# Two-layer attention kernel: the end of the first finished batch, the last stage and the bounds' check in another order, and its block of x1 asked for on another queue

## The chip, the core and the metric

The kernel runs on one core of one Trainium2 chip, in one launch. The metric is the device time of a run in microseconds (us); the median of several runs is compared. The trace of one profiled execution says what each engine did: TensorE (PE, with its weight loads as PEld), VectorE (DVE), ScalarE (ACT), GpSimd (POOL) and SyncE (SP), which here only issues DMAs.

## What is computed

The input x has two batches of 512 channels and 64 x 32 = 2048 tokens, in fp32. Cut to what matters (8 heads of 64):

```python
# layer 0
qk = concat([x, embedding])                  # 512 + 64 channels
q, k, v = qk @ Wq, qk @ Wk, x @ Wv           # tokens x 512
x1 = x + softmax(q k^T / 8) v @ Wout + bout  # full attention, 2048 x 2048 a head
# layer 1: attention by 256 landmarks (mean of 8 tokens each: qL, kL)
t = layer_norm(x1)
q, k, v = split(t @ Wqkv)
a1, a2, a3 = softmax(q kL^T), softmax(qL kL^T), softmax(qL k^T)
o = a1 @ (pinv(a2) @ (a3 @ v)) + conv33(v)   # pinv: 6 rounds of an iteration
t = x1 + o @ Wout + bout
out = t + layer_norm(t) @ (W @ dequantized).T
```

## The kernel before

Everything is kept with channels on the 128 partitions and tokens along the row: a batch is four blocks of 512 tokens (NTB = 4), each block four rows of channels (KC = 4). Heads go in pairs of two (NPAIR = 4 pairs a batch), so layer 1 has eight pairs; `todo` lists batch 1's four first, then batch 0's, and the text counts them n = 0 to 7.

**Order of work.** The instructions of PE, DVE, ACT and POOL run in the order in which the program writes them: each engine takes the next when its waits are met, and everything behind a waiting one on the same engine waits too. Only SP's order is the planner's. The program is written as generators that yield at places where something else may go between; `advance` (L793) takes one step of the next generator in a list, and a yielded `GAP` (`gap(n)` yields n of them) means that a generator sits out a turn, so that its next matmul isn't placed right behind the work that it needs. Results of matmuls go to PSUM banks; `bank` hands out four in turn, and a matmul into a bank waits for the reader of what stood there before.

**Layer 0's start** (L820 to 943). The weights and x are loaded on SP, the embedding (`emb_f`, 64 x 96) by two DMAs on POOL after VectorE has cleared it, and the embedding's weights (`we`) of the first chunk on ACT's queue. Twenty warm-up matmuls run meanwhile. For each of q and k of the first pair of heads, a matmul forms the embedding's part as 64 + 32 columns, VectorE copies it (`ft`, L888), POOL spreads it over 64 x 32 tokens (`e`, L889) and SP keeps it in memory (L895) for batch 1. VectorE adds e to each of the four projected blocks (L905). The buffer of e is one, for q and k in turn.

**Landmark scores** (`attend`, L1268). For each of the four pairs of a batch, two heads: two matmuls each into one half of a two-bank tile `sc2` (L1280), exp on ACT into X (L1287), sums and division on VectorE. POOL sets the last column of X to one (L1275). Pairs with i < 3 share one tile for the two heads.

**Pseudo-inverses** (the loop over `todo`, `pinv` at L1525). Five rounds of products of 256 x 256 matrices for two heads: a flip (a transpose at L1522 and a copy on ACT at L1523), products at L1532, combinations on VectorE (`less`, L1545), then three steps with transposed products (`wp` L1507, `tp` L1516). Each round is followed by `chunk(c)` and each of the last six half steps by `last(i)`: these put other work between, so that PE doesn't stand still. That other work is: for the pair before, the output of its four token blocks (`attn1_*`, L1581 to 1626: scores, exp, an addition `acc` L1598, values `av`, sums `rs`, a reciprocal L1618, a spread by eight DMAs on SP L790, a multiplication by it on VectorE L1625 and an addition to o on POOL L1626); for the pair after, its `attn3`, landmarks and start; the values of the pair after that; and `finish`.

**A batch's end** (`Finish1`, L1628; `finish1_units`, L1692). For each block t: x1 is read back into `xb` by four DMAs on SP (L1637). `out_units` project o (`yp`, L965) and add bias and x1 on VectorE (L972). `norm_units` takes the steps of `statistics` (L980): partial sums (L983, L984), a matmul for the mean and its subtraction `xn` (L988), squares on ACT (L991, L994) and their sums on VectorE (L996, L997), a matmul for the variance (L1000), root and reciprocal. `map_units` multiplies by the folded feed-forward map (`fp`, L1682), scales (L1671), adds (L1672) and stores each quarter on SP (L1673). Batch 1's blocks use one `xb` and one `xn` buffer, so block t + 1 can be read only when block t's four stores are done. Batch 1's end is appended to `finish` after pair n = 4 and is advanced in the chunks of pairs 5 to 7.

**The last stage.** After pair 7, a string (L2040) sets the order: `f` is a unit of batch 1's end, `1` a step of pair 7's output, `a` and `b` units of the projection of batch 0's blocks 0 and 1, `s` and `t` steps of their statistics. Batch 0's blocks have buffers of their own. Then the bounds' check: `halves` is set by three memsets on POOL (L2054 to 2056), a matmul sums the collected bounds (`bp`, L2058), three VectorE operations compare them and POOL reduces over the partitions (`bad`, L2064). At the very end `bad` is read (L2102, L2103), and if a bound is too large the whole is computed again in a safer way, which doesn't happen with these inputs. Last, batch 0's four blocks go through `map_units`, with the statistics of the next and the projection of the next but one between.

Of the kernel before, what the change touches and what calls it, by code (L numbers as in the profile page):

```python
# [663 lines left out]
def fast_path(  # L664
# [154 lines left out]


    emb_sb = wpool0.tile([64, H + W], F32, name="emb_f")
    nc.vector.memset(emb_sb, 0.0)
    w_sb = {kind: wpool0.tile([P, KC, C], F32, name=f"w{kind}_f") for kind in "qk"}
    we = {kind: wpool0.tile([64, C], F32, name=f"we{kind}_f") for kind in "qk"}

    def load_w0(kind, cols, queue=nc.sync):
        w = {"q": wq0, "k": wk0}[kind]
        nc.sync.dma_start(w_sb[kind][:, :, cols], chunked(w[:C, cols]))
        queue.dma_start(we[kind][:, cols], w[C:, cols])

    nc.gpsimd.dma_start(emb_sb[:32, :H], freq)
    nc.gpsimd.dma_start(emb_sb[32:, H:], time)
    load_w0("q", slice(0, P), nc.scalar)

    def load_x(src, b, name, first=0, n=NTB):
        tiles = []
# [21 lines left out]
    class Heads0:  # L858
# [12 lines left out]
        def embedded_and_projected(self, kind):  # L871

            cols, xbs = self.cols, self.xbs
            if kind == "q":
                self.q = qopool.tile([P, S], F32, tag="qo", name=f"q_{self.name}")

            def embedded(kind):


                e = wpool0.tile([P, H, W], F32, tag="e", name=f"e_{kind}_{self.name}")  # L880
                flat, kept = e.rearrange("p h w -> p (h w)"), e_d["qk".index(kind), self.hp]
                if self.b:
                    nc.sync.dma_start(flat, kept)
                    return flat
                fp = bank(f"fp_{kind}_{self.name}")
                nc.tensor.matmul(fp[:, : H + W], lhsT=we[kind][:, cols], rhs=emb_sb, start=True, stop=True)
                ft = wpool0.tile([P, H + W], F32, tag="ft", name=f"ft_{kind}_{self.name}")
                nc.vector.tensor_copy(ft, fp[:, : H + W])  # L888
                nc.gpsimd.tensor_tensor(  # L889
                    e,  # L890
                    ft[:, :H].unsqueeze(2).to_broadcast([P, H, W]),
                    ft[:, H:].unsqueeze(1).to_broadcast([P, H, W]),
                    ALU.add,
                )
                nc.sync.dma_start(kept, flat)  # L895
                return flat

            def project(kind, dst, e, t):
                toks = slice(t * TB, (t + 1) * TB)
                pp = bank(f"pp_{kind}_{self.name}_{t}")  # L900
                for k in range(KC):
                    nc.tensor.matmul(  # L902
                        pp, lhsT=w_sb[kind][:, k, cols], rhs=xbs[t][:, k, :], start=k == 0, stop=k == KC - 1
                    )
                nc.vector.tensor_tensor(dst[:, toks], pp, e[:, toks], ALU.add)  # L905

            dst = self.q if kind == "q" else self.k
            e = embedded(kind)
            if self.b:
                yield from gap(2)  # L910
            else:
                yield
                yield GAP
            for t in range(NTB):
                project(kind, dst, e, t)
                yield
# [60 lines left out]
    def deviation(name):  # L977
        return apool.tile([P, TB], F32, tag="rstd", name=f"rstd_{name}", bufs=1)

    def statistics(xb, xn, part, name, squares, row):  # L980


        nc.vector.tensor_tensor(part, xb[:, :2, :], xb[:, 2:, :], ALU.add)  # L983
        nc.vector.tensor_tensor(part[:, 0, :], part[:, 0, :], part[:, 1, :], ALU.add)  # L984
        yield
        mean = bank(f"mean_{name}")
        nc.tensor.matmul(mean, lhsT=mean_w, rhs=part[:, 0, :], start=True, stop=True)  # L987
        nc.vector.tensor_tensor(xn, xb, mean.unsqueeze(1).to_broadcast([P, KC, TB]), ALU.subtract)  # L988
        yield
        sq, *others = squares()  # L990
        nc.scalar.activation(sq, xn[:, :2, :], AF.Square)  # L991
        n = 2 // len(others)
        for i, other in enumerate(others):
            nc.scalar.activation(other, xn[:, 2 + i * n : 2 + (i + 1) * n, :], AF.Square)  # L994
            to = sq[:, i * n : (i + 1) * n, :]
            nc.vector.tensor_tensor(to, to, other, ALU.add)  # L996
        nc.vector.tensor_tensor(sq[:, 0, :], sq[:, 0, :], sq[:, 1, :], ALU.add)  # L997
        yield
        var = bank(f"var_{name}")
        nc.tensor.matmul(var, lhsT=mean_w, rhs=sq[:, 0, :], start=True, stop=True)  # L1000
        rstd = row()
        nc.scalar.activation(rstd, var, AF.Sqrt, bias=eps, scale=1.0)
        yield rstd
# [204 lines left out]
    class Pair:  # L1208
# [59 lines left out]
        def attend(self):  # L1268

            i, L = self.i, self.L  # L1270
            scs = scores_bank(f"sc2_{i}") if i + 1 < NPAIR else None
            X = self.X = [zpool.tile([P, 2, LM + 1], F32, tag=f"M{h}", name=f"X_{i}_{h}") for h in range(2)]
            rs = small.tile([P, 4], F32, tag="rs2", name=f"rs2_{i}")
            for h in range(2):
                nc.gpsimd.memset(X[h][:, :, LM:], 1.0)  # L1275
            for h in range(2):
                rows_h = slice(h * D, (h + 1) * D)
                sc = scs[:, h, :] if scs is not None else bank(f"sc2_{i}_{h}")
                for t in range(2):
                    nc.tensor.matmul(  # L1280
                        sc[:, t * LM : (t + 1) * LM],
# [346 lines left out]
    class Finish1:  # L1628

        def __init__(self, b, t, os, xb, xn):
            self.b, self.t, self.os, self.xb, self.xn = b, t, os, xb, xn
            self.name = f"g_{b}_{t}"
            toks = slice(t * TB, (t + 1) * TB)
            for m in range(KC):
                nc.sync.dma_start(xb[:, m, :], chunked(x1_d[b])[:, m, toks])  # L1637

        def out_units(self):
            return residual_units(self.b, self.t, self.xb, self.os, wo_sb, b1_sb, self.name)  # L1640

        def steps(self, row):
            def squares():
                sq = apool.tile([P, 2, TB], F32, tag="acc", name=f"sq_{self.name}")
                return sq, *(row_of(f"sq{k}_{self.name}").unsqueeze(1) for k in (2, 3))

            self.xn = self.xn()
            for rstd in statistics(self.xb, self.xn, self.xn[:, :2, :], self.name, squares, row):
                if rstd is not None:
                    nc.vector.reciprocal(rstd, rstd)  # L1650
                    self.rstd = rstd
                yield

        def norm_units(self):
            steps = self.steps(lambda: deviation(self.name))
            next(steps)
            yield GAP
            next(steps)
            yield
            next(steps)  # L1660
            yield from gap(2)
            next(steps)
# [29 lines left out]
    def finish1_units(b, os):  # L1692
        for t in range(NTB):
            xb = block_of(lpool, "xr", f"xb_g_{b}_{t}")
            f = Finish1(b, t, os, xb, lambda: block_of(lpool, "xn", f"xn_g_{b}_{t}"))
            yield from f.out_units()
            yield from f.norm_units()
            yield from f.map_units(lambda m, name: bank(name))
# [184 lines left out]
            next(first, None)  # L1883
    drain(first)
    todo[1].prefetch_w()
    vals = [values(1)]
    advance(vals)
    for n in todo[NPAIR - 1].front():
        advance(vals, n // 2)
    start_scale()  # L1890
    todo[0].prefetch1(kvpool.tile([P, S], F32, tag="k", name="q2_first"))


# [2 lines left out]
    for n, pair in enumerate(todo):  # L1896
# [20 lines left out]
        def chunk(c):  # L1917
            nonlocal landmarks
            if before and 0 < c <= n_ones:
                before.attn1_end(c - 1)  # L1920
            advance(finish)
            if c == NTB:
                if after:
# [64 lines left out]
        landmarks = start = None  # L1988
        n_ones = NTB if n + 2 < len(todo) else NTB - 1
        pair.pinv(chunk, last)  # L1990
        if n == NPAIR:
            finish.append(finish1_units(1, [p.o for p in todo[:NPAIR]]))

    def last_attn1():
        pair, ended = todo[-1], []
        for t in range(NTB):
            for j in range(2 if t else 0):
                pair.attn1_scores(t, j)
                if ended:
                    pair.attn1_end(ended.pop())  # L2000
                yield
            pair.attn1_add(t)
            pair.attn1_values(t)
            yield
            pair.attn1_sums(t)
# [10 lines left out]
        return Finish1(0, t, [p.o for p in todo[NPAIR:]], xb, xn)  # L2016


    fs = [last_block(t) for t in range(NTB)]

    def turns(units, *others):

        for other in others:
            next(units if other is None else other)
        drain(units)

    outs = [f.out_units() for f in fs]

    def deviation_of(t):
        def row():  # L2030
# [3 lines left out]
        return row  # L2034


    st = [f.steps(deviation_of(t)) for t, f in enumerate(fs)]

    ones_last = last_attn1()
    for c in "f1f1f1f1f1f1f1fa1a1a1as11bs1bs1bbt":  # L2040
        if c == "f":
            advance(finish)
        else:
            next({"1": ones_last, "a": outs[0], "b": outs[1], "s": st[0], "t": st[1]}[c])
    assert not finish
    drain(ones_last)
    todo[-1].attn1_end(NTB - 1)
    drain(outs[1])
    next(st[0])

    n = 3 * B * NPAIR

    halves = row_of("halves_f")[:, :P]
    nc.gpsimd.memset(halves, 0.0)  # L2054
    nc.gpsimd.memset(halves[:D, :D], 1.0)
    nc.gpsimd.memset(halves[D:, D:], 1.0)
    bp = bank("bp_f")
    nc.tensor.matmul(bp[:, :n], lhsT=halves, rhs=bound, start=True, stop=True)  # L2058
    ok = small.tile([P, n], F32, name="ok_f")
    nc.vector.tensor_scalar(ok, bp[:, :n], SAFE, None, ALU.is_lt)  # L2060
    oks = small.tile([P, 1], F32, name="oks_f")
    nc.vector.tensor_reduce(oks, ok, AX.X, ALU.min)
    nc.vector.tensor_scalar(oks, oks, -1.0, 1.0, ALU.mult, ALU.add)
    nc.gpsimd.partition_all_reduce(bad, oks, P, bass_isa.ReduceOp.max)  # L2064

    for t in range(NTB):
        maps = fs[t].map_units(wide_banks, 1 if t + 1 < NTB else 2)
        if t + 1 < NTB:
# [96 lines left out]
```

## Time and profile before

| what | value |
|---|---|
| median of 3 runs | 2764.85 us (2764.79 to 2766.75) |
| the profiled execution's own time | 2763.73 us |
| its span, first to last instruction | 2761.9 us |
| mean granted TensorE clock | 0.995 |
| busy: PE, PEld | 2703.8, 1363.3 us |
| busy: DVE, ACT, POOL | 1629.0, 905.8, 164.7 us |
| last matmul ends | 2754.09 us |
| x1 read back, quarter of a block (SP, 256 KB) | lands after 4.2 us |
| a whole block of 1 MB, from POOL | lands after 5.0 us |

The page gives each engine's busy time in the span, then groups of instructions by line. A line such as `L1084 DVE TENSOR_TENSOR acc_f<-acc_f,p_f ... x448 | 582.6, 1300 | 208.8 <-ACT ...` reads: line of the kernel, engine, operation, output and inputs, how many, then busy time in us and the mean of one in ns, then the engine's idle time just before them and what ended most of it. A view of waits lists, for an engine, what ended its idle time: the total, how often, the longest. A timeline gives start and length of each instruction in us from the span's start; idle time before it stands in brackets with what ended it. A stretch's line gives each engine's busy time in it and the TensorE clock that was granted, as a share of full speed.

### The profile page before, as it was taken

Reading aid. Unit: us, or ns where it says so; the run is one execution under the profiler, and the core shown is the slowest. Engines: PE = TensorE matmul, PEld = TensorE weight load, DVE = VectorE, ACT = ScalarE, POOL = GpSimd, SP = SyncE. Lnnn points to the kernel's source line nnn. Section 1 sums busy time; section 2 is a strip of 40 time slices with the busy share of each in tenths; the row PEclk is TensorE's granted clock in tenths of the full one; section 3 lists DMA queues with packets and bytes.
Section 4 is the critical chain, followed back from the end, with each engine's and each line's share of the span. In section 5 each row is a group of like instructions: output and inputs, shape, how many; then the busy total and the mean of one; then the engine's idle time right before and its main releaser. Section 6 shows DMA issues by size and latency. Waiting matters only on the chain. (4 is left out here: it accounts for less than half of the span.)

```text
span 2761.9 us, 41236 instructions
## 1 busy us (share of the span) xinstructions
PE 2703.8 (98%) x16994; PEld 1363.3 (49%) x16994; DVE 1629.0 (59%) x2068; ACT 905.8 (33%) x1352; POOL 164.7 (6%) x125
## 2 busy tenths in 40 slices
PE   9999999999999999999999999999999999899898
PEld 5343443434443334343344465777667767555334
DVE  2768787765558756657657444544644545556465
ACT  1434343433335334344512222223332323221210
POOL 1101101000001100000011000000000000000000
PEclk9999999999999999999999999999999999999999
DMA  4100000212111210021035532213111202111301
GB/s 145 42 9 24 28 20 26 83 35 69 32 66 54 96 39 9 21 73 41 24 107 187 187 121 90 95 32 126 43 36 59 81 9 90 40 64 31 107 31 47
DMA packets 112661, 174.00 MB, mean 63 GB/s; under 512 B 16320, under 2 KB 68048, under 8 KB 107856
## 3 DMA queue, kind: packets, MB, share of 16 engines
q1 hardware_dynamic: 107968, 154.46, 17.3%
q0 software_dynamic: 4416, 16.79, 1.6%
q8 instruction: 135, 2.21, 0.3%
q14 instruction: 62, 0.51, 0.1%
q10 hardware_dynamic: 80, 0.03, 0.0%
HBM read 90.87 MB, written 63.57 MB: 56 GB/s over the span
## 5 line engine op out<-in xcount | busy, mean ns | idle before, releaser
L1084 DVE TENSOR_TENSOR acc_f<-acc_f,p_f 128x1024 f32<-128x1024 f32 x448 | 582.6, 1300 | 208.8 <-ACT p_f L1074 180.2
L1074 ACT ACTIVATE p_f<-sc_f 128x1024 f32<-128x1024 f32 x512 | 496.4, 1021 | 564.2 <-PE sc_f L1066 561.5
L1066 PE MATMUL sc_f<-q_f,k_f 64*64 64x512 f32 x4096 | 491.1, 594 | 2.7 <-ACT p_f L1074 2.7
L1096 PE MATMUL av_f<-p_f,v_f 64*64 64x512 f32 x4096 | 484.3, 589 | 0.0
L1096 PEld LDWEIGHTS av_f<-p_f,v_f 64*64 64x64 f32 x4096 | 156.5, 133 | 283.0 <-issue 283.0
L1066 PEld LDWEIGHTS sc_f<-q_f,k_f 64*64 64x64 f32 x4096 | 145.8, 133 | 285.6 <-issue 262.0
L1239 PE MATMUL pp<-xh,w 128*128 128x512 f32 x512 | 231.0, 603 | 0.7 <-ACT q L1242 0.7
L1239 PEld LDWEIGHTS pp<-xh,w 128*128 128x128 f32 x512 | 95.8, 192 | 122.2 <-issue 115.0
L1532 PE MATMUL pb<-R 128*128 128x192 f32 (+1 forms) x640 | 151.1, 383 | 1.6 <-DVE M L1545 1.6
L1532 PE MATMUL pa<-M 128*128 128x192 f32 (+1 forms) x640 | 150.7, 380 | 0.1
L950 PEld LDWEIGHTS vp_f<-wv_f,x 128*128 128x128 f32 x1024 | 115.7, 192 | 13.5 <-issue 11.8
L950 PE MATMUL vp<-w,xh 128*128 128x128 f32 x1024 | 120.8, 276 | 0.0
L950 PEld LDWEIGHTS vp<-w,xh 128*128 128x128 f32 x1024 | 117.0, 192 | 7.2 <-issue 4.2
L1532 PEld LDWEIGHTS pb<-R 128*128 128x128 f32 x640 | 107.7, 192 | 25.1 <-DVE M L1545 2.3
L950 PE MATMUL vp_f<-wv_f,x 128*128 128x128 f32 x1024 | 118.7, 277 | 0.0
L1532 PEld LDWEIGHTS pa<-M 128*128 128x128 f32 x640 | 108.0, 193 | 21.0 <-ACT M L1523 2.5
L902 PE MATMUL pp_q_f<-x,wq_f 128*128 128x512 f32 x256 | 114.4, 599 | 2.1 <-DVE q_f L905 1.4
L965 PE MATMUL yp_g<-o,wo_f 128*128 128x512 f32 x256 | 115.5, 598 | 0.8 <-DVE y_g L1671 0.8
L902 PE MATMUL pp_k_f<-x,wk_f 128*128 128x512 f32 x256 | 114.3, 599 | 1.7 <-DVE k_f L905 1.3
L1682 PE MATMUL fp_g<-xn_g,mT 128*128 128x512 f32 (+1 forms) x264 | 115.7, 589 | 0.0
L965 PE MATMUL yp_f<-q_f,wo_f 128*128 128x512 f32 x256 | 113.7, 598 | 0.9 <-DVE xr_f L972 0.9
L1114 POOL TENSOR_TENSOR q_f<-q_f,rinv_f 128x512 f32<-128x512 f32 x32 | 44.4, 1387 | 1041.9 <-DMA rinv_f<-acc_f 850.7
(196 smaller groups left out, 2719.3 us busy)
## 6 DMA issues: line engine op xcount, KB each, us to landing
xh<-xh_fd SPq DMA_DIRECT2D x12, 1024.0 KB, 5.6
rinv_f<-acc_f SPq DMA_DIRECT2D x256, 32.0 KB, 1.8
xr_f<-in_x_dram SPq DMA_DIRECT2D x8, 1024.0 KB, 5.2
x_fd<-xr_f POOLq DMA_DIRECT2D x8, 1024.0 KB, 5.0
xh_fd<-xn_f POOLq DMA_DIRECT2D x8, 1024.0 KB, 4.6
k_fd<-k SPq DMA_DIRECT2D x32, 256.0 KB, 2.6
q_fd<-q SPq DMA_DIRECT2D x32, 256.0 KB, 3.1
xb_g<-x_fd SPq DMA_DIRECT2D x32, 256.0 KB, 4.2
```

The lines of the kernel that those rows point to most:

```text
L902: nc.tensor.matmul(pp, lhsT=w_sb[kind][:, k, cols], rhs=xbs[t][:, k, :], start=k == 0, stop=k == KC - 1)
L950: nc.tensor.matmul(vp[:, j * P : (j + 1) * P], lhsT=xb[:, k, j * P : (j + 1) * P], rhs=w_of(k), start=k == 0, stop=k == KC - 1,)
L965: nc.tensor.matmul(yp, lhsT=wo_sb[:, k, m * P : (m + 1) * P], rhs=oTs[k][:, toks], start=k == 0, stop=k == NPAIR - 1,)
L1066: nc.tensor.matmul(sc[r * D : (r + 1) * D, h, :], lhsT=hd.k[rows, lo : lo + D], rhs=hd.q[rows, t * TB : (t + 1) * TB], start=True, stop=True,)
L1074: nc.scalar.activation(p, sc, AF.Exp, scale=D**-0.5)
L1084: nc.vector.tensor_tensor(acc, first if c == 1 else acc, p, ALU.add)
L1096: nc.tensor.matmul(av[r][half, :], lhsT=hd.v[keys, c, half], rhs=pp[keys, h, :], start=c == 0, stop=c == NST - 1,)
L1114: nc.gpsimd.tensor_tensor(o, o, rinv, ALU.mult)
L1239: nc.tensor.matmul(pp, lhsT=self.w[j][:, c, :], rhs=xhs[t][:, c, :], start=c == 0, stop=c == KC - 1)
L1532: nc.tensor.matmul(dst, lhsT=lhsT[:, k, t * P : (t + 1) * P], rhs=rhs[:, k, :], start=k == 0, stop=k == 1)
L1682: nc.tensor.matmul(fp[:, cols], lhsT=mT[:, k, m * P : (m + 1) * P], rhs=self.xn[:, k, cols], start=k == 0, stop=k == KC - 1,)
```

## The change

1. **Start.** `emb_f` is cleared only in the two quarters that no DMA writes. The first chunk of wq, `we` and the embedding's two DMAs all go to ACT's queue, in this order (before: SP, ACT and POOL).
2. **e** of the first pair of heads of batch 0 (for q and for k) is made by VectorE rather than by POOL.
3. **Statistics** get `apart`, used by batch 1's end: a yield between the squares on ACT and their additions on VectorE, and all of ACT's squares are issued before the first addition.
4. **attend** takes two score tiles, one for each head, for i < 3, and X's last column is set by VectorE.
5. **Batch 1's end** reads a block of x1 by one DMA of 1 MB on POOL, and sits out two turns before its projection. The turns sat out in `norm_units` are moved: two after the partial sums, one after the squares.
6. **Order.** Batch 1's end begins in chunk 1 of pair 4 rather than after pair 4. The string of the last stage is another; a letter `n` in it makes batch 0's last blocks with their reads of x1, and the addition `acc` of pair 7's output comes right after its scores.
7. **The bounds' check** moves from the end to around `start_scale`, before the loop over the pairs: memsets before the last values and `front`, matmul and VectorE operations before `start_scale`, the reduction right after it.

```diff
--- before.py
+++ after.py
@@ -819,18 +819,19 @@
 
 
     emb_sb = wpool0.tile([64, H + W], F32, name="emb_f")
-    nc.vector.memset(emb_sb, 0.0)
+    nc.vector.memset(emb_sb[:32, H:], 0.0)
+    nc.vector.memset(emb_sb[32:, :H], 0.0)
     w_sb = {kind: wpool0.tile([P, KC, C], F32, name=f"w{kind}_f") for kind in "qk"}
     we = {kind: wpool0.tile([64, C], F32, name=f"we{kind}_f") for kind in "qk"}
 
     def load_w0(kind, cols, queue=nc.sync):
         w = {"q": wq0, "k": wk0}[kind]
-        nc.sync.dma_start(w_sb[kind][:, :, cols], chunked(w[:C, cols]))
+        queue.dma_start(w_sb[kind][:, :, cols], chunked(w[:C, cols]))
         queue.dma_start(we[kind][:, cols], w[C:, cols])
 
-    nc.gpsimd.dma_start(emb_sb[:32, :H], freq)
-    nc.gpsimd.dma_start(emb_sb[32:, H:], time)
     load_w0("q", slice(0, P), nc.scalar)
+    nc.scalar.dma_start(emb_sb[:32, :H], freq)
+    nc.scalar.dma_start(emb_sb[32:, H:], time)
 
     def load_x(src, b, name, first=0, n=NTB):
         tiles = []
@@ -886,7 +887,9 @@
                 nc.tensor.matmul(fp[:, : H + W], lhsT=we[kind][:, cols], rhs=emb_sb, start=True, stop=True)
                 ft = wpool0.tile([P, H + W], F32, tag="ft", name=f"ft_{kind}_{self.name}")
                 nc.vector.tensor_copy(ft, fp[:, : H + W])
-                nc.gpsimd.tensor_tensor(
+
+                engine = nc.gpsimd if self.b or self.hp else nc.vector
+                engine.tensor_tensor(
                     e,
                     ft[:, :H].unsqueeze(2).to_broadcast([P, H, W]),
                     ft[:, H:].unsqueeze(1).to_broadcast([P, H, W]),
@@ -977,7 +980,7 @@
     def deviation(name):
         return apool.tile([P, TB], F32, tag="rstd", name=f"rstd_{name}", bufs=1)
 
-    def statistics(xb, xn, part, name, squares, row):
+    def statistics(xb, xn, part, name, squares, row, apart=False):
 
 
         nc.vector.tensor_tensor(part, xb[:, :2, :], xb[:, 2:, :], ALU.add)
@@ -992,6 +995,9 @@
         n = 2 // len(others)
         for i, other in enumerate(others):
             nc.scalar.activation(other, xn[:, 2 + i * n : 2 + (i + 1) * n, :], AF.Square)
+        if apart:
+            yield
+        for i, other in enumerate(others):
             to = sq[:, i * n : (i + 1) * n, :]
             nc.vector.tensor_tensor(to, to, other, ALU.add)
         nc.vector.tensor_tensor(sq[:, 0, :], sq[:, 0, :], sq[:, 1, :], ALU.add)
@@ -1268,14 +1274,14 @@
         def attend(self):
 
             i, L = self.i, self.L
-            scs = scores_bank(f"sc2_{i}") if i + 1 < NPAIR else None
+            scs = [scores_bank(f"sc2_{i}_{h}")[:, 0, :] for h in range(2)] if i + 1 < NPAIR else None
             X = self.X = [zpool.tile([P, 2, LM + 1], F32, tag=f"M{h}", name=f"X_{i}_{h}") for h in range(2)]
             rs = small.tile([P, 4], F32, tag="rs2", name=f"rs2_{i}")
             for h in range(2):
-                nc.gpsimd.memset(X[h][:, :, LM:], 1.0)
+                nc.vector.memset(X[h][:, :, LM:], 1.0)
             for h in range(2):
                 rows_h = slice(h * D, (h + 1) * D)
-                sc = scs[:, h, :] if scs is not None else bank(f"sc2_{i}_{h}")
+                sc = scs[h] if scs else bank(f"sc2_{i}_{h}")
                 for t in range(2):
                     nc.tensor.matmul(
                         sc[:, t * LM : (t + 1) * LM],
@@ -1629,34 +1635,40 @@
 
 
 
-        def __init__(self, b, t, os, xb, xn):
+        def __init__(self, b, t, os, xb, xn, t_by_t=False):
             self.b, self.t, self.os, self.xb, self.xn = b, t, os, xb, xn
             self.name = f"g_{b}_{t}"
             toks = slice(t * TB, (t + 1) * TB)
+            if t_by_t:
+
+                nc.gpsimd.dma_start(xb, chunked(x1_d[b])[:, :, toks])
+                return
             for m in range(KC):
                 nc.sync.dma_start(xb[:, m, :], chunked(x1_d[b])[:, m, toks])
 
         def out_units(self):
             return residual_units(self.b, self.t, self.xb, self.os, wo_sb, b1_sb, self.name)
 
-        def steps(self, row):
+        def steps(self, row, apart=False):
             def squares():
                 sq = apool.tile([P, 2, TB], F32, tag="acc", name=f"sq_{self.name}")
                 return sq, *(row_of(f"sq{k}_{self.name}").unsqueeze(1) for k in (2, 3))
 
             self.xn = self.xn()
-            for rstd in statistics(self.xb, self.xn, self.xn[:, :2, :], self.name, squares, row):
+            for rstd in statistics(self.xb, self.xn, self.xn[:, :2, :], self.name, squares, row, apart):
                 if rstd is not None:
                     nc.vector.reciprocal(rstd, rstd)
                     self.rstd = rstd
                 yield
 
         def norm_units(self):
-            steps = self.steps(lambda: deviation(self.name))
+            steps = self.steps(lambda: deviation(self.name), True)
+            next(steps)
+            yield from gap(2)
+            next(steps)
+            yield
             next(steps)
             yield GAP
-            next(steps)
-            yield
             next(steps)
             yield from gap(2)
             next(steps)
@@ -1692,7 +1704,8 @@
     def finish1_units(b, os):
         for t in range(NTB):
             xb = block_of(lpool, "xr", f"xb_g_{b}_{t}")
-            f = Finish1(b, t, os, xb, lambda: block_of(lpool, "xn", f"xn_g_{b}_{t}"))
+            f = Finish1(b, t, os, xb, lambda: block_of(lpool, "xn", f"xn_g_{b}_{t}"), True)
+            yield from gap(2)
             yield from f.out_units()
             yield from f.norm_units()
             yield from f.map_units(lambda m, name: bank(name))
@@ -1883,11 +1896,26 @@
             next(first, None)
     drain(first)
     todo[1].prefetch_w()
+
+
+    halves = row_of("halves_f")[:, :P]
+    nc.gpsimd.memset(halves, 0.0)
+    nc.gpsimd.memset(halves[:D, :D], 1.0)
+    nc.gpsimd.memset(halves[D:, D:], 1.0)
     vals = [values(1)]
     advance(vals)
     for n in todo[NPAIR - 1].front():
         advance(vals, n // 2)
+    n_bounds = 3 * B * NPAIR
+    bp = bank("bp_f")
+    nc.tensor.matmul(bp[:, :n_bounds], lhsT=halves, rhs=bound, start=True, stop=True)
+    ok = small.tile([P, n_bounds], F32, name="ok_f")
+    nc.vector.tensor_scalar(ok, bp[:, :n_bounds], SAFE, None, ALU.is_lt)
+    oks = small.tile([P, 1], F32, name="oks_f")
+    nc.vector.tensor_reduce(oks, ok, AX.X, ALU.min)
+    nc.vector.tensor_scalar(oks, oks, -1.0, 1.0, ALU.mult, ALU.add)
     start_scale()
+    nc.gpsimd.partition_all_reduce(bad, oks, P, bass_isa.ReduceOp.max)
     todo[0].prefetch1(kvpool.tile([P, S], F32, tag="k", name="q2_first"))
 
 
@@ -1918,6 +1946,9 @@
             nonlocal landmarks
             if before and 0 < c <= n_ones:
                 before.attn1_end(c - 1)
+            if n == NPAIR and c == 1:
+
+                finish.append(finish1_units(1, [p.o for p in todo[:NPAIR]]))
             advance(finish)
             if c == NTB:
                 if after:
@@ -1988,18 +2019,18 @@
         landmarks = start = None
         n_ones = NTB if n + 2 < len(todo) else NTB - 1
         pair.pinv(chunk, last)
-        if n == NPAIR:
-            finish.append(finish1_units(1, [p.o for p in todo[:NPAIR]]))
 
     def last_attn1():
         pair, ended = todo[-1], []
+        pair.attn1_add(0)
         for t in range(NTB):
             for j in range(2 if t else 0):
                 pair.attn1_scores(t, j)
                 if ended:
                     pair.attn1_end(ended.pop())
+                if j:
+                    pair.attn1_add(t)
                 yield
-            pair.attn1_add(t)
             pair.attn1_values(t)
             yield
             pair.attn1_sums(t)
@@ -2016,15 +2047,11 @@
         return Finish1(0, t, [p.o for p in todo[NPAIR:]], xb, xn)
 
 
-    fs = [last_block(t) for t in range(NTB)]
-
     def turns(units, *others):
 
         for other in others:
             next(units if other is None else other)
         drain(units)
-
-    outs = [f.out_units() for f in fs]
 
     def deviation_of(t):
         def row():
@@ -2034,35 +2061,23 @@
         return row
 
 
-    st = [f.steps(deviation_of(t)) for t, f in enumerate(fs)]
-
     ones_last = last_attn1()
-    for c in "f1f1f1f1f1f1f1fa1a1a1as11bs1bs1bbt":
+    for c in "11ffnf11f1ff1afafff1f1f1f1faas11bs1bs1bbt":
         if c == "f":
             advance(finish)
+        elif c == "n":
+
+            fs = [last_block(t) for t in range(NTB)]
+            outs = [f.out_units() for f in fs]
+
+            st = [f.steps(deviation_of(t)) for t, f in enumerate(fs)]
         else:
-            next({"1": ones_last, "a": outs[0], "b": outs[1], "s": st[0], "t": st[1]}[c])
+            next(ones_last if c == "1" else {"a": outs[0], "b": outs[1], "s": st[0], "t": st[1]}[c])
     assert not finish
     drain(ones_last)
     todo[-1].attn1_end(NTB - 1)
     drain(outs[1])
     next(st[0])
-
-    n = 3 * B * NPAIR
-
-    halves = row_of("halves_f")[:, :P]
-    nc.gpsimd.memset(halves, 0.0)
-    nc.gpsimd.memset(halves[:D, :D], 1.0)
-    nc.gpsimd.memset(halves[D:, D:], 1.0)
-    bp = bank("bp_f")
-    nc.tensor.matmul(bp[:, :n], lhsT=halves, rhs=bound, start=True, stop=True)
-    ok = small.tile([P, n], F32, name="ok_f")
-    nc.vector.tensor_scalar(ok, bp[:, :n], SAFE, None, ALU.is_lt)
-    oks = small.tile([P, 1], F32, name="oks_f")
-    nc.vector.tensor_reduce(oks, ok, AX.X, ALU.min)
-    nc.vector.tensor_scalar(oks, oks, -1.0, 1.0, ALU.mult, ALU.add)
-    nc.gpsimd.partition_all_reduce(bad, oks, P, bass_isa.ReduceOp.max)
-
     for t in range(NTB):
         maps = fs[t].map_units(wide_banks, 1 if t + 1 < NTB else 2)
         if t + 1 < NTB:
```

## The prediction

> **What bounds the kernel now.** I read the page first: the engines' shares, then the waits of TensorE, the chain of work that ended last, and the timelines around each gap. The first line of the page:
>
> ```profile
> PE 2703.8 (98%) x16994; PEld 1363.3 (49%) x16994; DVE 1629.0 (59%) x2068; ACT 905.8 (33%) x1352; POOL 164.7 (6%) x125
> ```
>
> TensorE is busy for 2703.8 of 2761.9 us, so the work itself leaves 58 us to win: about 50 in gaps and 7.8 after the last matmul (2754.09). The change adds and removes no matmul. So only TensorE's idle time counts, and the view of its waits lists it (total, times, longest):
>
> ```profile
> PE p_pb L1522 <- DVE R L1545: 7.2, 2, 6.8
> PE sc L1280 <- ACT X L1287: 6.2, 3, 3.5
> PE rs L779 <- DVE acc L1598: 5.1, 1, 5.1
> PE bp_f L2058 <- POOL halves_f L2056: 4.9, 1, 4.9
> PE mean_g L987 <- DVE xn_g L984: 3.0, 1, 3.0
> PE wp L1507 <- DVE R L1545: 2.4, 2, 1.6
> PE pp_q_f L902 <- DVE q_f L905: 1.4, 2, 0.9
> PE pp_k_f L902 <- DVE k_f L905: 1.3, 1, 1.3
> ```
>
> The first names VectorE, but its timeline shows that VectorE itself stood still for a load of x1 (idle before it in brackets):
>
> ```profile
> 2389.65 0.75 DVE L972 SCALAR_TENSOR_TENSOR xb_g<-yp_g,b_f,xb_g 128x512 f32<-128x512 f32 x1 [10.39 <-DMA xb_g<-x_fd]
> 2390.32 0.74 DVE L1545 SCALAR_TENSOR_TENSOR R<-M,pa 128x320 f32<-128x320 f32 x2
> ```
>
> A gap costs more than itself. In stretches of 4 us (fields after the engines: TensorE's clock, then DMA), after the gaps of 6.8, 5.1 and 4.9:
>
> ```profile
> 2391.00:2395.00 4.00, 3.55 (x9) 2.67 (x10) 2.05 (x7) 0.27 (x1) 0.00 (x0) 0.50 0.00 2
> 2395.00:2399.00 4.00, 4.00 (x16) 2.53 (x15) 2.11 (x5) 0.27 (x1) 0.30 (x1) 0.99 0.00 2
> 2596.00:2600.00 4.00, 3.17 (x12) 0.86 (x14) 2.39 (x2) 1.70 (x3) 0.00 (x0) 0.57 0.93 354
> 2664.00:2668.00 4.00, 3.69 (x7) 1.63 (x8) 1.97 (x4) 0.00 (x0) 0.22 (x2) 0.59 0.00 0
> ```
>
> Half clock for about 3.4 us is 1.7 us lost. All six gaps of 2.0 us or more (at 1489.6, 1528.8, 2384.1, 2520.5, 2591.8, 2659.4: 3.5, 2.0, 6.8, 3.0, 5.05, 4.95) show it; none up to 1.58 does. Together they hold 25.2 us of idle time and 10.5 of slow clock. The last is in the chain:
>
> ```profile
> 2661.65 0.70 DVE rinv L1625
> ...
> 2662.48 1.25 POOL o L1626
> 2663.73 0.15 POOL halves_f L2054
> ...
> 2664.31 0.40 PE bp_f L2058 x2
> 2664.72 5.22 PE fp_g L1682 x8
> ```
>
> The check's matmul waits for three memsets that queue on POOL behind an addition, which waits for a DMA; the eight matmuls behind it take 5.22 us, where such eight take 3.43 at full clock.
>
> [...] here L988 (128x2048, one operand broadcast) takes 2.28. [...] In the trace x1's block costs four issues of 0.43 us on SP and lands 4.2 us after one; 1 MB from POOL takes 5.0.
>
> **Start** (page, POOL and VectorE timelines). e for q takes 3.63 us on POOL, 12.84 to 16.46, though its input is ready at 8.69. On VectorE, idle there, it ends near 8.7 + 2.3 = 11.0, long before TensorE wants the bank at 16.30: the gap of 0.94 goes. e for k can't start before the store of the first lands (29.21); on VectorE it ends at 31.5 rather than 32.84, and its addition at 32.2, before TensorE needs the bank at 32.29: 1.33 goes. wq, we and the embedding move to ACT's queue, and x is asked for one issue earlier on SP; the bytes are the same, so the 0.60 for x stays. If the embedding, now fourth on its queue, landed after the warm-up (7.94) it would cost; it has some 4 us. Sum -2.3 (-2.9 to -0.5).
>
> **Attend** (three pairs). The second head's scores wait for the first head's exp in the same tile, behind a key copy, two squares and a table load of 1.28 on ACT. Two tiles end that. The gaps are 0.7, 3.5 + 1.7 and 2.0 + 1.7. In the second the next matmul, the variance, needs VectorE's chain, which runs without a break until 1496.84; I take a third of it, -1.7 (-0.8 to -2.6). With -0.7 and -3.7: -6.1 (-7.5 to -4). The two memsets of X cost VectorE about 0.1 each, beside its slack.
>
> **Bounds' check.** At the end -4.95 and -1.65; the matmul's 0.4 moves along. In its new place it is followed by TensorE's 64 value matmuls (1739.2 to 1746.3), while the matrix it waits for is ready at 1742.7: 3.6 us cover the three small VectorE operations (0.5) and the reduction on POOL (0.38). With that cover gone they would cost 0.9. Its memsets are issued early, past no waiting work. Next at its old place are the map's matmuls, whose input is done. -6.6 + 0.2 = -6.4 (-6.8 to -5.5).
>
> **Finish.** From 2300 on, the check apart, TensorE loses 23.9 us idle (28.8 - 4.95) and 5.4 in slow clock: 29.3. The change starts batch 1's end earlier by most of a pair, spreads its steps (squares apart from their additions, the mean two units after its input), and asks for x1 with one DMA on POOL, no longer behind SP's eight spreads (0.63 each). Gone: 6.8 + 2 for the load (it should land about 4 us before its addition), 1.06, 1.58, 0.8, most of 3.0 + 1.7 and of 5.05 + 1.7. But TensorE has no slack anywhere, so each new step makes something else late. Walking the new order with the durations of before (product 1.84, mean subtraction 2.28, squares 1.06 + 1.13, additions 1.29 + 0.69, spread 6.3 from reciprocal to landing), I find: between pairs 4 and 5, 2.8 (a bank held until the mean is subtracted; the flip's copy on ACT behind squares); pair 5, 0.45 and 1.7 at its end; pair 6, 0.5; pair 7's first chunk, 3.7 + 1.7: block 2's load waits for the last store of block 1 (2.6), then issue and landing (0.8 + 5.0), and what is ahead on POOL, about 10 in all, its addition is due at 5.5, and VectorE's products queue behind it; the rest of pair 7, 1.4 + 1.5 + 3.9; the last stage, 1.75 and 2.35 + 1.7. Sum 23.5, so -5.8. POOL's output additions (1.26) queue behind a waiting load too; the matmuls they feed come later than the block's. The ends of this term are 0 and -18: the walk is rough, each stall being a difference of two sums.
>
> **Sum.** -2.3 - 6.1 - 6.4 - 5.8 = -20.6 against the profiled execution's 2763.73 (span 2761.9), so 2743.1; the median of the runs, 2764.85, is 1.1 higher, so I forecast 2744.2.
>
> **Rivals.**
> A, most of the new waits hide: the finish gains 18, in all -33, 2732. For it: each wait in my list is under 3 us but one, and banks are four. Against: 98% busy leaves nothing to slide.
> B, half clock: five waits I put at 1.4 to 2.8 without slow clock grow by half a microsecond each and trip it, 5 x 2.2 = 11 back: -9.6, 2755. For it: 2.0 us is enough to trip. Against: those of 1.06 to 1.58 in the trace don't.
> C, slower: the loads on POOL's queue. One DMA waits for all four stores of the block before, where SP asked quarter by quarter; VectorE stands at L972 until it lands, TensorE behind it. I have 5.4 + 1.85 for blocks 2 and 3 and nothing for block 1. To undo 20.6, the three must cost 27.9, 9.3 each: 7.4 idle and 1.9 in slow clock. With 10 us from store to landing, each addition would have to be due within 2.6 us of the last store. Past that point it is slower; at 1 us it is 2770. Against: two empty units are put ahead of the additions, and only one of three looks tight.
> D, no difference: both B's slow clock and two of C's late loads (2 x 3.7 more): -20.6 + 11 + 7.4 = -2.2, 2763, if the finish is tight everywhere at once. Against: B and C have each their own argument against them.
>
> **Numbers.** My sum 0.50 (2738 to 2750), A 0.22, B 0.18, D 0.06, C 0.04. Faster by over 0.2% (5.5 us, about what a measurement can tell from no change) 0.90, within it 0.06, slower 0.04. Range 2730 to 2757, which leaves out C, D and the far ends of A and B.
>
> **What would show it.** e on VectorE at 8.7 and no wait of L902 but x's; no wait of L1280 on L1287; no `bp_f` among the waits and no half clock in the last 90 us but once or twice; no VectorE wait of 10 us for x1 near block 1, one of about 4 near block 2. Wrong would be an L972 that waits over 7 us for every block, or over four new stretches at half clock.

## The result, and the profile after

The changed kernel takes 2745.59 us (median of 4 runs, 2742.82 to 2746.37), the kernel before 2765.8 (4 runs, 2764.79 to 2768.34): a ratio of 0.9924, 95% interval 0.991 to 0.9938. The forecast was 2744.2. The profiled execution took 2746.23, with a span of 2744.4 against 2761.9, so the two traces differ by 17.5 us of the 20. The page's line of the engines after the change:

```profile
PE 2698.0 (98%) x16994; PEld 1361.6 (50%) x16994; DVE 1631.3 (59%) x2087; ACT 905.5 (33%) x1352; POOL 161.1 (6%) x109
```

TensorE has the same 16994 instructions, yet 5.8 us less busy time. What it loses to slow clock (busy time in each stretch, times what the granted clock lacked) fell from 10.3 to 6.0 us; another 3.2 us come from matmuls that now overlap, as will be seen; small pieces elsewhere go the other way. Its waits after (total, times, longest):

```profile
PE p_pb L1528 <- DVE R L1551: 5.4, 2, 3.7
PE var_n L1006 <- issue: 3.7, 1, 3.7
PE fp_g L1694 <- DVE rinv L1631: 3.2, 1, 3.2
...
PE yp_g L968 <- DVE xb_g L975: 2.3, 1, 2.3
```

Set beside the list of before: the waits for exp (6.2), for `acc` (5.1) and for `halves_f` (4.9) are gone, that for the mean's input went from 3.0 to 0.3 and that for R from 7.2 to 5.4. New are 3.7 at a variance, 3.2 at the map's first matmul and 2.3 at a projection. Lining up the same ScalarE copies in both traces gives where the 17.5 went: 0.9 in layer 0's start, 7.0 in attend, nothing between, and the rest, 9.6, from the end of pair 4 on.

The forecast's largest new wait stands where it was put, at block 2 of batch 1. VectorE's timeline:

```profile
2476.39 0.75 DVE L975 SCALAR_TENSOR_TENSOR xb_g<-yp_g,b_f,xb_g 128x512 f32<-128x512 f32 x1 [7.56 <-DMA xb_g<-x_fd]
```

and POOL's, where the load waits for the last of block 1's four stores, then takes 0.77 to issue and 4.7 more to land (2476.20; the addition begins 0.19 us later):

```profile
2470.74 0.77 POOL L1644 DMA_DIRECT2D xb_g<-x_fd  x1 [16.58 <-DMA out_dram<-xb_g]
```

TensorE's wait is 3.73, where 3.7 was forecast. The wait that was not forecast stands where the check had been. The chain after the change:

```profile
2641.36 1.67 DVE acc L1624
...
2647.44 1.84 DMA rinv<-acc
...
2649.45 0.70 DVE rinv L1631
2650.16 0.14 issue
2650.29 3.67 PE fp_g L1694 x8
```

The check's memsets and its matmul are gone from it, but what stood above them stays: reciprocal, spread, multiplication by rinv. TensorE waits 3.16 us.

### The profile page after: what moved, and what is told of

The parts are those of the page before. It is cut to its first block, busy times and chain, and to the rows that moved or that the text cites. A ratio compares the mean times of both kernels' runs of the same rounds, so it can differ in the third digit from the quotient of the medians.

```text
span 2744.4 us, 41181 instructions
## 1 busy us (share of the span) xinstructions
PE 2698.0 (98%) x16994; PEld 1361.6 (50%) x16994; DVE 1631.3 (59%) x2087; ACT 905.5 (33%) x1352; POOL 161.1 (6%) x109
## 4 chain that ended last, share of the span: by engine, by line
PE 90%; DVE 5%; DMA 2%; SPq 1%; ACT 1%; issue 1%; POOL 0%; DVEq 0%; POOLq 0%; ACTq 0%
PE sc_f L1072 15%; PE av_f L1102 15%; PE pp L1245 8%; PE pb L1538 5%; PE pa L1538 5%; PE vp_f L953 4%; PE vp L953 4%; PE fp_g L1694 4%; PE pp_k_f L905 4%; PE yp_f L968 4%; PE pp_q_f L905 3%; PE yp_g L968 3%; PE sc L1367 2%; PE av L1388 2%; PE sc L1595 2%; DVE acc_f L1090 2%
```

## The experiments

All times are medians; ratios are to the kernel before. Theory and rival are in each expectation. The first four put one part of the change into the kernel before.

**The bounds' check alone** (part 7 of the diff, nothing else).

> The kernel before with part 7 alone, the bounds' check moved ahead of the loop. Forecast's term: -6.4 us, with the gap of 4.95 and the slow clock behind it gone. Theory after the result: the map's first matmul at the old place also waits for the bank that the last multiplication by rinv (L1625 in the kernel before) reads, so a gap of 4.95 becomes one of about 3.2 with that release, and the time falls by 1.8 + 0.4 for the matmul, some 2.2, or up to 3.9 if the slow clock stays away. In the new place it costs under 0.1.

Measured: 2766.82 us, ratio 1.0001 (0.9992 to 1.0009). TensorE's timeline in place of the 4.95:

```profile
2665.47 1.02 PE L1000 MATMUL var_g<-sq_g,mean_w 128*128 128x512 f32 x2
2669.60 5.37 PE L1682 MATMUL fp_g<-xn_g,mT 128*128 128x512 f32 x8 [3.11 <-DVE rinv L1625]
```

The wait is 3.11 and the eight matmuls behind it still take 5.37 (5.22 before): 1.8 us of idleness gone, the slow clock kept. In its new place the check costs at most 0.2. The forecast's -6.4 fell. The theory's gap of about 3.2 is there; its gain of 2.2 us is at the very edge of what the time allows (-2.2 to +2.5). The profiled execution can't show it either: it took 2769.36, the longest of the 13, with 5.2 us more slow clock than the trace of before, all of it ahead of the check's old place.

**The two score tiles alone** (part 4).

> The kernel before with part 4 alone, two score tiles. Forecast's term: -6.1 us. Theory after the result: -7.0, of which 1.4, 0.8 and 4.8 at the three pairs; no wait of L1280 for the exp, and in the second pair a wait of about 3.7 at the variance matmul in the place of the 3.5.

Measured: 2757.87 us, ratio 0.9967 (0.9955 to 0.9979), so -9.1 (-12.4 to -5.8). The wait of 3.69 at the variance is there. Of the 7.0 us by which attend is shorter in the traces, idle time gives 2.1 and slow clock 1.7 (one stretch rather than two). The other 3.2 are in TensorE's timeline of the kernel before (third pair) and of this one:

```profile
1527.67 1.13 PE L1280 MATMUL sc<-L,L 64*128 64x256 f32 x4
1530.81 1.41 PE L1280 MATMUL sc<-L,L 64*128 64x256 f32 x4 [2.02 <-ACT X L1287]
```

```profile
1526.13 1.14 PE L1280 MATMUL sc<-L,L 64*128 64x256 f32 x8
1527.20 7.13 PE L1239 MATMUL pp<-xh,w 128*128 128x512 f32 x16
```

Four and four one after the other take 1.13 + 1.41; eight together take 1.14. Each head's matmuls use 64 of the array's 128 rows (`64*128`, where others show `128*128`), and where the second didn't wait, both heads ran in the time of one. Where no exp came between, the eight took 1.14 in the kernel before too (at 1596.71). Over the kernel the group at L1280 falls from 12.9 to 9.1 us busy; 0.5 of this is slow clock, the rest some 1.1 us at each of three pairs. Neither forecast nor theory counted this overlap (1.14 for eight, 1.13 for four).

**The start alone** (parts 1 and 2).

> The kernel before with parts 1 and 2 alone. Forecast's term: -2.3 us. Theory after the result: -0.9, since the second block of x is asked for 2.0 us later (SP stands from 2.5 to 5.2 us for a DMA semaphore that two more DMAs on the hardware queues have taken), so a wait of about 0.8 stays at the second projection of q, and e for k still waits for the store of e for q, so 1.0 stays there. The time alone can't tell 0.9 from 2.3; the gaps in the trace can.

Measured: 2763.73 us, ratio 0.9991 (0.9984 to 0.9998), so -2.5 (-4.4 to -0.6). In the trace both waits are there about as the theory has them (1.15 and 0.85). But one pair of traces is little to go by: layer 0's first value matmul starts between 40.60 and 43.41 us in the four kernels with the old start, and between 39.17 and 41.64 in the ten traces with the new, 1.7 earlier on average. POOL's beginning of e for q wanders most, as in the trace of the two score tiles alone (its input was ready at 8.27):

```profile
14.98 3.62 POOL L889 TENSOR_TENSOR e_q_f<-ft_q_f 128x2048 f32<-128x2048 f32 x1 [12.14 <-issue]
29.85 3.63 POOL L889 TENSOR_TENSOR e_k_f<-ft_k_f 128x2048 f32<-128x2048 f32 x1 [11.25 <-DMA e_fd<-e_q_f]
```

With the check alone it began at 8.55, in the kernel before at 12.84. Yet this isn't what decides: in all fourteen traces e for k begins when the store of e for q has landed (28.96 to 30.17, whether e for q was done at 10.8 or at 18.6), and the first value matmul starts 7.8 us after e for k ends, or about 9.5 in the two traces with a stretch of slow clock there. With the check alone, where e for q began first, the value matmul comes last (43.41). What VectorE saves is that e for k takes 2.29 rather than 3.63 us. The time doesn't tell 0.9 from 2.3.

**The end alone** (parts 3, 5 and 6).

> The kernel before with parts 3, 5 and 6 alone, the order of batch 1's end and of the last stage; the bounds' check stays at the end. Forecast's term: -5.8 us. Theory after the result: what is left of -17.5 in the profiled runs once 0.9, 7.0 and the check's 2.2 to 3.9 are taken off, so -5.7 to -7.4, with the check's gap of about 5 still there, block 2's wait for x1 of 3.7 on TensorE, and none at block 1. If the parts are not additive, it is here that it shows.

Measured: 2757.44 us, ratio 0.9967 (0.9955 to 0.9979), so -9.1 (-12.4 to -5.8): more than the theory's -5.7 to -7.4 at the middle, within the interval. From 2300 on, idle time falls from 28.8 to 19.7, or to 22.1 with the waits of pair 4 that the earlier begin brings; slow clock falls from 6.8 to 4.2. The check's gap is still 4.95. The four ratios add up to -0.74%, the whole change is -0.76%: this agrees with parts that are additive, though each ratio is known to about 0.1% only. Parts 3, 5 and 6 were not run apart.

The next four change one thing in the changed kernel.

**The map's first bank.**

```diff
-        return product_bank(name) if m % 2 else side_bank(1 + m, name)
+        return product_bank(name) if m % 2 else side_bank(3 - m, name)
```

> The changed kernel with one thing altered: the map's even quarters take the two side banks in the other order, so that the first matmul after the last block's projection goes to a bank that nobody reads. Theory (the bank of the last values held the first map's matmul, and the check's memsets stood in front of that wait): the gap of 3.16 before the first fp goes, 1.5 to 3.2 us less than the changed kernel, 2742 or so. Rival (the gap is the arrival of rinv itself, which the matmul needs some other way): the gap stays and so does the time.

Measured: 2739.2 us, ratio 0.9903 (0.9888 to 0.9919). The gap is gone:

```profile
2641.05 1.02 PE L1006 MATMUL var_g<-sq_g,mean_w 128*128 128x512 f32 x2
2641.91 3.60 PE L1694 MATMUL fp_g<-xn_g,mT 128*128 128x512 f32 x8
```

So it was a bank that the last values still held, not the data. The change of the median is larger, 6 us, though the two intervals of the ratio overlap. In the two profiled executions the rest is 1.7 us of slow clock at the variance in attend, which this one doesn't have, and 3.1 at block 3's projection (0.96 idle here, 2.35 and 1.7 of slow clock there).

**x1 by quarters**, `for m in range(KC)` with `xb[:, m, :]` in place of the one DMA, on POOL and on SP.

> The changed kernel with x1 of batch 1's blocks read by four DMAs of 256 KB on POOL rather than one of 1 MB. Theory (the one DMA waits for the last of the four stores, so the block's first addition waits 7.6 us on VectorE and TensorE 3.7): the first quarter lands earlier, the gap at block 2 falls below 1 us and its slow clock goes, -3 to -5 us, 2741 or so. Rival (each issue on POOL costs 0.8 us and lands no earlier, since POOL reaches it late): the gap stays, 0 to +2 us.

> As the last, with the four DMAs on SP. Theory (it is the single DMA that costs, not the queue): like the four on POOL within 2 us, as long as the planner doesn't put them behind the eight spreads of a reciprocal. Rival (the queue matters, as the change has it: SP's order puts the loads behind spreads that wait for VectorE): a gap of 5 us or more comes back at one of blocks 1 to 3, +3 us or more over the four on POOL.

Measured: 2737.71 us on POOL (0.99, 0.9885 to 0.9916), 2738.88 on SP (0.9903, 0.9888 to 0.9918). Block 2's gap falls to 1.89 and 1.16, not below 1. The reason given was half wrong: on POOL the first quarter is not asked for before the last store,

```profile
2468.74 2.15 POOL L1645 DMA_DIRECT2D xb_g<-x_fd  x4 [16.54 <-DMA out_dram<-xb_g]
```

but the first addition follows 3.84 us after this, not 5.65 as with 1 MB. No gain of the queue is seen: SP does as well within 2 us, and no gap of 5 comes back.

**The embedding on POOL's queue**, `nc.gpsimd` for its two loads.

> The changed kernel with the embedding's two DMAs on POOL's queue again. Theory (two more DMAs on the hardware queues use up the eight semaphores, so that SP stands from 2.5 to 5.2 us before it asks for wk and the second block of x): SP issues wk at about 2.6 and x at about 3.7, and the second projection of q starts 0.5 to 0.8 earlier. Rival (the second block is late because the data is, not the request): SP asks earlier, TensorE's gap stays. The time can't tell; at most 1 us.

SP's timeline in the changed kernel, then here:

```profile
0.72 1.81 SPq L846 DMA_DIRECT2D x<-in_x_dram  x4
5.24 0.39 SPq L829 DMA_DIRECT2D wk_f<-in_wk_dram  x1
...
6.29 1.68 SPq L840 DMA_DIRECT2D x<-in_x_dram  x3
```

```profile
0.72 1.81 SPq L846 DMA_DIRECT2D x<-in_x_dram  x4
2.57 0.43 SPq L829 DMA_DIRECT2D wk_f<-in_wk_dram  x1
...
5.32 1.49 SPq L840 DMA_DIRECT2D x<-in_x_dram  x3
```

Measured: 2744.15 us, 0.9922 (0.9908 to 0.9935). SP no longer stands still ahead of wk, x comes 1.0 earlier (not 2.6, since the next semaphore is still awaited), and the wait at the second projection is gone. Of the time it can't be told.

The last four ran on one chip.

**The changed kernel again.**

> The changed kernel once more, for the comparison with the three below on one chip: 2743 to 2746.5 us. Theory (the same gap costs 1.7 us of slow clock in one execution and nothing in the next, by its place in the clock's window): idle gaps within 0.3 us of the first trace at each place but the start, and slow clock that differs by steps of about 1.7. Rival (the gaps themselves differ between executions): gaps differ by over 0.5 us at places other than the start and x1's load.

Measured: 2745.8 us (2743.68 to 2748.83), 0.9925 (0.9912 to 0.9939). The gaps agree within 0.05 us (3.68, 3.76, 3.17 at the three largest), but for the start and the wait at block 3's projection (1.06 in place of 2.35). The latter is x1's load again, which took 6.2 us from issue to landing here and 7.3 there; so the rival, which leaves that load out, fell, and the theory's "each place but the start" was too narrow. The slow clock cost 6.0 and 6.3 us in all, in other places. The traces also show the clock's window: within each of the fourteen, all stretches at half clock begin on one grid of 3.413 us. Two windows of this grid around the same gap at the map's first matmul, in the changed kernel (3.16) and then with the check alone (3.11):

```profile
2645.19:2648.60 3.41, 1.94 (x5) 0.57 (x3) 2.22 (x3) 0.69 (x1) 0.00 (x0) 1.00 0.20 48
2648.60:2652.01 3.41, 1.72 (x4) 0.87 (x5) 3.01 (x3) 0.00 (x0) 1.26 (x1) 1.00 0.07 17
```

```profile
2666.72:2670.13 3.41, 0.53 (x2) 0.32 (x3) 3.02 (x4) 0.49 (x1) 0.54 (x1) 1.00 0.12 29
2670.13:2673.54 3.41, 3.41 (x6) 1.34 (x5) 2.59 (x1) 0.00 (x0) 0.73 (x1) 0.50 0.03 7
```

In the first the gap is shared by two windows, 1.47 and 1.69 us of idleness, and the clock stays full. In the second 2.88 us fall into one window, and the next is at half clock.

**Bounds' operations later**: the five VectorE operations at the end of `keys_and_queries` are put in a function that `attend` calls last.

> The changed kernel with the bounds' five small VectorE operations after a pair's keys and queries (2.5 us in all) moved behind attend's sums. Theory (at the second pair attend's two tiles gain almost nothing since VectorE's chain to the variance ends last, with these five in it): the wait of 3.69 at the variance falls to about 1.2, with no slow clock: -2.5 to -4.2 us. Rival (the chain is bound by ACT's squares or the reciprocal): the wait stays above 3.

Measured: 2742.61 us (2742.3 to 2747.64), 0.992 (0.9907 to 0.9934): not to be told from the changed kernel. The wait fell to 2.37 only, and that at the first pair's mean rose from 0.37 to 1.29. VectorE and POOL show why:

```profile
1490.86 0.67 DVE L1253 TENSOR_REDUCE big<-k 128x1 f32<-128x512 f32 x1
1491.45 2.19 DVE L1002 TENSOR_TENSOR xr_f<-xr_f 128x1024 f32<-128x1024 f32 x1
```

```profile
1489.24 3.33 POOL L1025 TENSOR_TENSOR xn_f<-xn_f,rstd_n 128x1024 f32<-128x1024 f32 x1 [19.32 <-DVE rstd_n L1023]
```

The addition takes 2.19 rather than 1.21: it ends 1.1 us after POOL's multiplication does (1492.57), about its own length. Theory and rival both missed.

**Three of them, and all four.**

> The changed kernel with the embedding on POOL's queue, the map's other bank and x1 by quarters on POOL together. Theory (three separate waits, no one behind the other): the gaps of 3.16 and at the second projection of q are gone, block 2's is 1.9, 5.5 us less idle than the changed kernel and up to 4 of slow clock: 2736 us (2734 to 2739). Rival (a gap that goes in one place makes another later): 2739 or more, with a new gap of over 1 us after block 2's.

> The same three with the bounds' five operations moved too. Theory: 2.5 to 4.2 below the three, 2733 us (2730 to 2736), and hardly a gap of 2 us left, so a clock of 0.999 or more. Rival: no better than the three by more than 1 us.

Measured: 2737.06 us for the three (0.9891, 0.9876 to 0.9906), 2735.78 for all four (0.9884, 0.9869 to 0.9899), against 2745.8 on the same chip. The gaps of the three went as expected (block 2's is 1.74). One wait over 1 us is new, 1.30 at pair 7's scores, which stand behind VectorE's addition of block 3's x1; it comes in place of 0.68 there and 1.06 at block 3's projection. Idle time from 2200 on fell from 20.8 to 15.1 (gaps of 0.12 us and more), so the waits were in the main separate ones. The fourth adds 1.3, within the spread, which is its rival's side. The intervals of both lie below that of the changed kernel.

## Why the prediction was right, and where it was not

The sum was right (-20.6 forecast; -20.2 by the medians), and in part by luck: the check's term was 6.4 too much, and attend and finish, timed alone, gave 3.0 and 3.3 more than forecast at the middle of their intervals. Between the two traces the difference is 17.5 only.

- **Start**, -2.3: -0.9 in the profiled pair, -2.5 (-4.4 to -0.6) timed. Two steps failed. "x is asked for one issue earlier on SP" holds for x's first four DMAs (0.72 instead of 1.22 us); the next were asked for 2.0 later. In the trace the DMAs of SP's and ACT's queues count on eight semaphores in turn. With x's four and ACT's four, wk is the ninth: SP waits 2.7 us ahead of it for wq's load, the first of ACT's, and issues it at 5.24, when that load has landed (5.22). The embedding alone on POOL removes this wait (wk at 2.57). And the gains at e for q and e for k (0.94 and 1.33) don't add up: e for k did wait at 29.6 for the store, as forecast, but with the 0.94 gone TensorE wanted the bank at 31.67, not at 32.29, and waited 1.05 there.
- **Attend**, -6.1: -7.0 in the traces, -9.1 (-12.4 to -5.8) timed. "The change adds and removes no matmul. So only TensorE's idle time counts" failed: the heads' matmuls now overlap, 3.2 us of busy time. The second pair gained 0.8, the low end given, but not as forecast: its wait grew from 3.47 to 3.69, and the overlap made up for it.
- **The check**, -6.4: 0 (-2.2 to +2.5). The step "next at its old place are the map's matmuls, whose input is done" failed. The input was; the bank was not. The chain that the forecast shows has the multiplication by rinv end at 2662.35, and the gap's start, 2659.4, is 3.0 before it: the 3.16 could be read there. I took the last of two waits for the only one.
- **Finish**, -5.8: -9.1 (-12.4 to -5.8). The list of new waits held well: 3.7 was 3.73, 1.75 was 1.56, 2.8 at the border of pairs 4 and 5 was 2.1 (0.68 and 1.43), 0.45 and 1.7 in pair 5 were 0.36 and 1.20; 2.35 + 1.7 at the last variance was 1.50 without slow clock. Most were a little too long, and none of those under 2 us paid slow clock in this trace. Block 3 was mis-sized the other way: 1.85 forecast, 2.35 + 1.7 measured, or 1.06 in the second trace. The mis-sized term is the sum of new waits and slow clock, 23.5 forecast: with the end alone, the check's gap and its slow clock left out, it is 17.1 + 1.4.
- **Slow clock.** That every gap of 2.0 us or more costs 1.7 was too simple. The wait of 3.69 at the variance cost 1.7 in six traces and nothing in two, that of 3.1 to 3.4 at the map's first matmul nothing in five and 1.7 in two, a gap of 3.47 in attend between 1.7 and 3.4, and one of 1.74 and one of 1.76 cost 1.7, where two of 1.89 cost nothing. What tells the cases apart in the traces is how much idleness, small gaps included, falls into one window of the grid. Of the windows at full clock in the fourteen traces, from 10 us on, all 37 with more than 2.02 us of idleness were followed by half clock, 8 of the 31 with 1.65 to 2.02, and none with less. (Matmuls' ends are modelled in the trace, so the border is not sharp.) So about 2 us of idleness in a window of 3.413 were enough in these traces. No run here moves a gap against the grid on purpose. That it also makes the 3.5 us between runs of one kernel, together with the start, is likely and not shown.

Of the rivals, A's 18 us at the end did not come, and D neither. C had its mechanism: VectorE stood for x1 at block 2 (7.6 us, where the forecast named about 4 as a sign) and at block 3 (8.2, which the profile puts down to a spread; the block's own load landed at 2567.92, 0.19 before the addition, as at block 2). The quarters show that the size of the load costs it, not the queue (block 2's gap 1.89 on POOL and 1.16 on SP in place of 3.73). B's five waits, that at block 3's projection (2.35) apart, stayed under 2 us.

What stays open: how much of the timed gains above the traces' (2 us in attend) is clock; why the median with the check alone shows nothing of the 1.8 us; which of parts 3, 5 and 6 the end's gain comes from; and why POOL began e for q so late in three of four traces, for which the trace says only "issue". A candidate for the last, not tested: POOL has two MODIFY_POOL_CONFIG of L889 at 2.9 us in the trace of before, and the same pair at 2664.45 is followed by the reduction of the check after 5.91 us of "issue".

## What to carry to other kernels

A wait that the profile names is the last of several. Before its removal is counted, follow the chain one release further up, and look at the bank or buffer as well as at the data: what is left over is the difference of the two, here 1.8 of 4.95 us. When two gaps in a row go, the second must be reckoned anew, since the engine comes to it sooner. A term that comes from one pair of traces needs a second trace of before: the start alone moved by 2.8 us between executions. And a wait between matmuls that would else run at once, as the two heads' here, costs the overlap too, beside the idle time: some 1.1 us at each of three pairs.

## What was not expected of the hardware

- VectorE operations with two inputs took longer beside POOL's multiplication of 128x1024 in two places. In the trace of before, at 1492.14, a multiplication of 128x1 by 128x1 takes 1.58 us beside it; with POOL idle (bounds' operations later) the same takes 0.15. The short one ends with the long one (1493.72 and 1493.70). The reductions just ahead of it, with one input and beside the same POOL instruction, take 0.15 for one and 0.73 for two. The other place is the addition of 2.19 rather than 1.21 above. What holds VectorE up the traces don't show. A VectorE multiplication of 128x1024 that had begun 0.11 us ahead of POOL's took no more than 1.23.
- In the fourteen traces the slow clock came in stretches of 3.413 us on a grid that is fixed within a trace: 1.7 us lost in each that is busy (TensorE busy for 3.41 at a granted clock of 0.50 at 2670.13 with the check alone). Idle stretches of 2 to 3.7 us cost none, one or two of them: the 3.73 at block 2 was followed by two, the 3.69 at the variance by one in six traces and by none in two. That it depends on how the stretch lies on the grid is read from the idleness in each window (2.88 us in one window, then half clock; 1.47 and 1.69 in two, then none).
